# Row norms of a gated network's last layer split in two steps, and the first scores of an attention moved in front of other products

## The chip, the core and the metric

The kernel runs on one core of one Trainium2 chip. A core has five engines with a queue each: TensorE (PE, matrix products; its weight loads are listed apart as PEld), VectorE (DVE), ScalarE (ACT), GpSimd (POOL) and SyncE (SP, which here only issues DMAs). Each engine is given its instructions in an order that is fixed when the program is built; where one needs the result of another engine, it waits. The metric is the time on the device in microseconds (us) of one execution; the figure is the median of several runs.

## What is computed

The reference is a two-layer network on x of shape (8, 256, 512). Each layer adds a gated cross-attention on a context and then a gated feed-forward block, each behind a layer norm:

```python
x = x + tanh(g_xattn[0]) * _L0_xattn_ref(_layernorm(x), ctx, ctx)
x = x + tanh(g_ffn[0])   * _L0_ffn_ref(_layernorm(x), ...)
x = x + tanh(g_xattn[1]) * _L1_xattn_ref(_layernorm(x), ctx, ...)
x = x + tanh(g_ffn[1])   * _L1_ffn_ref(_layernorm(x), ...)
```

The change touches the second layer only. Its attention projects the queries (a linear with bias, then an RMS norm) and runs a softmax attention of 16 heads of 32 over 256 keys of each of the 8 batches. Its feed-forward block norms a row once more, rounds it to 8 bits with a scale from the row's largest magnitude, multiplies it with ternary weights, forms `value * silu(gate)`, rounds that in the same way and projects it back:

```python
h  = x * rsqrt(mean(x * x) + EPS) * w_norm
gv = _bitlinear(h, w_gv)            # scale from max(abs(h)) of each row
out = _bitlinear(value * silu(gate), w_out)
return x + out
```

## The kernel before

The 2048 rows of x are 16 tiles of 128 rows, two for each of the 8 batches (blocks b = 0 to 7). The program has three parts: the preparation of layer 0's weights with layer 1's keys and values, then layer 0's feed-forward, then layer 1's feed-forward. Each part interleaves the attention of later or earlier blocks with its own work. The last part, from about 750 us on, is the one that the change touches.

**How the order is set.** Every step (a Python function that issues some instructions) gets a place by hand: `at(b, (n, step))` puts it at block b plus n/16, and `timeline` (L617) issues all steps in the order of their places. One block of layer 1 is 16 places long, one for each `glu` step. On TensorE this written order is kept exactly: `pe.held` (L860) chains each matmul behind the one before. On the other engines a planner in the compiler reorders: it plays the program through in its own model of time and lets each engine take, of the instructions that it believes ready, the one written first. `behind(ins, last)` (L301) adds an order between two instructions of one engine, with no semaphore; the planner must then keep them in that order.

**What one block does** (places in sixteenths of a block, in the repeating middle):

- `Feed1.glu(k)` (L1252), places 0 to 15: eight steps for each of the two tiles. A step multiplies the tile's transposed 8-bit rows (zT) into a PSUM bank pair, which ACT copies to `gv` (L1269). Every second step ACT forms a tanh (L1273, tile `t`), and DVE does three instructions: L1274 and L1276 (the tile `u`) and L1277 (its largest magnitude).
- `Feed1.done` (L1309), from 8.6 for the first tile and 17.4 (so 1.4 of the next block) for the second: the scale (L1286 to L1289, small DVE instructions), two ACT instructions on `u` (L1315), two on POOL (L1316), DMA transposes (L1321), and 16 matmuls into a bank `py`. The first tile of a block uses the bank named "o" for it, the second the one named "py". `store` (L1302) adds the result to x (L1306 on DVE), which frees the bank, and sends the rows out. The first tile's second half of these matmuls stands at 18.2, so at 2.2 of the next block.
- `Feed1.ready` (L1211), norms of the next block's tiles, written as one step `norm` at 10.3 (first tile) and 13.0 (second) and a step `turn` 1.7 later. `norm` takes the moments on DVE, two reciprocal roots on POOL (through `rsqrt`, L269), y and z on POOL (L1220, L1226); then on DVE the row's largest magnitude (`amax`, L1228), the scale (L1229 to L1231) and the rounding (L1233, and L1234 to `zq`); then on POOL the residual (L1236, L1237) and three 128x1 products (`back`, L1242 to L1244). `turn` sends zq through a transposing DMA on SP into zT.
- `Attention1.ready` (L1050), three blocks ahead: a layer norm at 3.6, its transposes at 12.2, the queries' first linear (`normed.first(0)`) at 14.2, the second at 16.2 (0.2 of the next block; 15.6 for the first such attention), their scale at 0.5, the loads of keys and values at 1.0 and the transposes to `qT` at 2.9. Both linears write the one bank "py", one after the other: the second can't start before DVE has added the bias of the first (L756), and ACT squares the sum (L757) behind it. The transposes go to a PSUM pair `turned`, which ACT copies to qT (L348).
- `Attention.looks`, two blocks ahead: for each of four groups of heads, `scores(g)` runs the products of qT and kT (16 matmuls of 32 rows, into two PSUM pairs) and takes their negated maxima with two DVE reductions (L419, `nm`). The places are 4.4, 6.4, 7.4 and 9.3; `parts` and `shift` follow at 10.4 and 14.1.
- `Attention.weighs`, one block ahead: `exps(g)` (scores again, the other way round, with the maxima added, then ACT's exponentials at L485) at 15.2 of the block before, 1.2, 3.4 and 5.6, and `weigh(g)` (products with the values, into the bank "o") at 3.2, 4.2, 6.2 and 7.2.
- `Attention1.done`: 7.3 to 11.2, the division by the sums and the output projection.

The PSUM pairs with the tag "s" are two buffers in turn: `turned` takes one, and `scores` and `exps` take both. All matmuls have line L257 and all of these transposes L260, since `Tensor` issues them; they are told apart by their tiles. "s<-kT,qT" is `scores`, "s<-qT,kT" is `exps`.

The last three blocks differ: from block 5 on no new queries are begun, from block 6 on there are no more scores, and block 7's tiles are normed at 7.7 and 8.4 of block 6.

Of the kernel before, what the change touches and what calls it, by code (L numbers as in the profile page):

```python
# [45 lines left out]
ALU = mybir.AluOpType  # L46
AX = mybir.AxisListType
# [40 lines left out]
def flamingo_kernel(  # L88
# [24 lines left out]
    nc = tc.nc  # L113
# [32 lines left out]
    def want(i, n):  # L146
        assert stage.get(i, 0) == n, (i, n)
# [48 lines left out]
    for g in range(DC):  # L196
        for i in range(2):
            at = SR * g + SR // 2 * i
# [63 lines left out]
    pe = Tensor()  # L262

    exp = [None]


    block = {}
# [33 lines left out]
    def behind(ins, last):  # L301

        if last is not None:
            tc.add_manual_dep(
                ins.ins,
                last.ins.name,
                mybir.DependencyInfo(mybir.DependencyClass.NoSync, mybir.DependencyReason.DATA),
                reason="behind",
            )
        return ins  # L310
# [31 lines left out]
    def turned(srcs, dst):  # L342

        t = pair((P, 2, DC, P), name="turned")
        for i, src in enumerate(srcs):
            for c in range(DC):
                pe.transpose(t[:, i, c, :], src[:, c * P : (c + 1) * P], ident)
        nc.scalar.copy(dst.rearrange("p c (i t) -> p i c t", i=2), t)  # L348
# [13 lines left out]
    class Attention:  # L362
# [3 lines left out]
        n = 0  # L366
# [185 lines left out]
    class Attention0(Attention):  # L552
# [3 lines left out]
        def ready(self):  # L556
            def load():
                self.kT = self.new("kT", [DC, S])
                nc.sync.dma_start(out=self.kT, in_=cxT[self.b].rearrange("(c p) s -> p c s", p=P))
                self.v = self.new("v", [2, D])  # L560
                nc.sync.dma_start(out=self.v, in_=cx[self.b].rearrange("(k p) d -> p k d", p=P))

            def norm():

                rows = [xs[2 * self.b], xs[2 * self.b + 1]]
                self.y = layernorm(rows, att, "y", float(HD), block.get("V"))

            def turn():
                self.qT = self.new("qT", [DC, S])
                turned(self.y, self.qT)  # L570

            return self.counted(0, [load, norm, turn])
# [52 lines left out]
    def at(b, *steps):  # L625

        return [(b + n / 16, b + n / 16, [step]) for n, step in steps]
# [116 lines left out]
    def normed(src, w, bias, nw, dst, pool, tag, out2):  # L744

        st = {}

        def first(i):
            if i == 0:
                st["ss"] = small.tile([P, 2], F32, tag="ss", name="ss")  # L750
                st["t"] = []
                st["out"] = out2()
            t = pool.tile([P, D], F32, tag=tag, name="lin", bufs=YB)
            out = st["out"](i)
            linear(out, src(), i, w)
            nc.vector.tensor_tensor(t, out, bias(), ALU.add)  # L756
            nc.scalar.activation(junk, t, AF.Square, accum_out=st["ss"][:, i : i + 1])  # L757
            st["t"].append(t)

        def scale():  # L760
            r = rsqrt(st["ss"], 2, 1.0 / D, 1e-6)
            for i, t in enumerate(st["t"]):
                if nw is None:
                    nc.gpsimd.tensor_scalar(t, t, r[:, i : i + 1], 0.0, ALU.mult, ALU.add)
                else:
                    nc.vector.scalar_tensor_tensor(t, t, r[:, i : i + 1], nw(), ALU.mult, ALU.mult)

        def turn():
            turned(st["t"], dst())

        return [lambda: first(0), lambda: first(1), scale, turn]
# [48 lines left out]
    with ExitStack() as part:  # L820
# [16 lines left out]
        jobs = []  # L837
# [3 lines left out]
        for b in range(B):  # L841
            load, k0, k1, scale, turn, store, v0, v1 = kv[b]
# [280 lines left out]
    with ExitStack() as part:  # L1123
# [4 lines left out]
        def rows(b):  # L1128
# [3 lines left out]
        jobs = [  # L1132
            (0.5, 3.0, [lambda u=u: measure1(u) for u in range(n1)]),
            (3.05, 3.05, [scales1]),
            (3.1, 6.5, [lambda u=u: quantize1(u) for u in range(n1)]),
            (6.6, 6.6, [hold1]),
            (3.0, 3.0, [load_queries]),
        ]
# [66 lines left out]
    class Feed1:  # L1205
# [3 lines left out]
            self.i = i  # L1209

        def ready(self):  # L1211
            def norm():
                xt = xs[self.i]
                want(self.i, 3)
                mv = moments([xt])
                m, var = mv[:, 0, 0:1], mv[:, 0, 1:2]
                r = rsqrt(var, 1, 1.0, LN_EPS)[:, 0:1]
                nc.vector.tensor_scalar_mul(m, m, -1.0)
                y = work.tile([P, D], F32, tag="yr", name="yr", bufs=2)
                nc.gpsimd.tensor_scalar(y, xt, m, r, ALU.add, ALU.mult)  # L1220

                v2 = small.tile([P, 1], F32, tag="v2", name="v2")
                nc.vector.scalar_tensor_tensor(v2, r, r, var, ALU.mult, ALU.mult)
                r2 = rsqrt(v2, 1, 1.0, 1e-5)[:, 0:1]
                z = work.tile([P, D], F32, tag="z", name="z", bufs=2)
                nc.gpsimd.tensor_tensor(z, y, nw, ALU.mult)  # L1226
                amax = small.tile([P, 1], F32, tag="amax", name="amax")
                nc.vector.tensor_reduce(amax, z, AX.X, ALU.max, apply_absolute_value=True)  # L1228
                nc.vector.tensor_tensor(amax, amax, r2, ALU.mult)  # L1229
                sc, inv = scale8(amax)  # L1230
                nc.vector.tensor_tensor(sc, sc, r2, ALU.mult)  # L1231
                self.zq = work.tile([P, D], BF, tag="zq", name="zq", bufs=2)
                nc.vector.tensor_scalar(z, z, sc, MAGIC, ALU.mult, ALU.add)  # L1233
                nc.vector.tensor_scalar_add(self.zq, z, -MAGIC)  # L1234

                nc.gpsimd.tensor_scalar(y, y, tg[:, 3:4], 0.0, ALU.mult, ALU.add)  # L1236
                nc.gpsimd.tensor_tensor(xt, xt, y, ALU.add)  # L1237


                self.back = small.tile([P, 3], F32, tag="back", name="back")  # L1240
                back = self.back
                nc.gpsimd.tensor_tensor(back[:, 0:1], inv, winv[:, 0:1], ALU.mult)  # L1242
                nc.gpsimd.tensor_tensor(back[:, 1:2], inv, whalf, ALU.mult)
                nc.gpsimd.tensor_tensor(back[:, 2:3], back[:, 0:1], back[:, 1:2], ALU.mult)  # L1244

            def turn():
                self.zT = work.tile([P, DC, P], BF, tag="zT", name="zT", bufs=3)
                nc.sync.dma_start(out=self.zT, in_=self.zq, transpose=True)

            return [norm, turn]  # L1250

        def glu(self, k):  # L1252
            if k == 0:
# [30 lines left out]
        def scale(self):  # L1284
            amax = small.tile([P, 1], F32, tag="amax", name="amax")
            nc.vector.tensor_reduce(amax, self.amax, AX.X, ALU.max)  # L1286
            nc.vector.tensor_tensor(amax, amax, self.back[:, 2:3], ALU.mult)
            sc, self.inv = scale8(amax)
            nc.vector.tensor_tensor(sc, sc, self.back[:, 2:3], ALU.mult)  # L1289
            self.uq = work.tile([P, HID], BF, tag="uq", name="uq", bufs=1)  # L1290
            return sc
# [69 lines left out]
    jobs = []  # L1361
    for b in range(B):
        first, second, a = feed1[2 * b], feed1[2 * b + 1], att1[b]
        end = b == B - 1
        jobs += at(b, *((k, step) for k, step in enumerate(first.glus() + second.glus())))

        far = {B - 1: (15.95, 15.95), B - 2: (15.95, 15.95), B - 3: (13.2, 17.3)}.get(b, (13.2, 18.2))
        steps = {B - 1: (7.05, 7.1, 7.15), B - 2: (7.4, 9.6, 9.8)}.get(b, (8.6, 9.6, 9.8))
        jobs += at(b, *zip((*steps, *far), first.done()))
        if end:  # L1370
            jobs += at(b, (16.0, second.last))
        else:
            far = {B - 2: (31.9, 31.9), B - 3: (21.2, 22.2)}.get(b, (21.2, 24.2))
            jobs += at(b, *zip((17.4, 18.4, 18.6, *far), second.done()))
        if b >= 2:

            late = 15.6 if b == 2 else 16.2
            jobs += at(b - 3, *zip((3.6, 12.2, 14.2, late, 16.5, 17.0, 18.9), a.ready()))
            jobs += at(b - 2, *zip((4.4, 6.4, 7.4, 9.3, 10.4, 14.1), a.looks()))
        if b >= 1:  # L1380
            steps = (-0.8, 0.6, 2.3, 2.5, 3.2, 3.4, 4.2, 5.0) if end else (-0.8, 1.2, 3.2, 3.4, 4.2, 5.6, 6.2, 7.2)
            jobs += at(b - 1, *zip(steps, a.weighs()))
        steps = (5.1, 6.9, 7.6, 8.2) if end else (7.3, 9.2, 10.2, 11.2)
        jobs += at(b - 1, *zip(steps, a.done()))
        for n, f in zip((7.7, 8.4) if end else (10.3, 13.0), (first, second)):
            norm, turn = f.ready()
            jobs += at(b - 1, (n, norm), (n + 1.7, turn))
    timeline(*jobs)


# [50 lines left out]
```

## Time and profile before

| | |
|---|---|
| median of 3 runs | 1191.43 us (1191.4 to 1193.26) |
| the profiled execution's own time | 1192.33 us |
| its span, first to last instruction | 1190.6 us |
| mean granted TensorE clock | 0.987 |
| PE busy in the span | 1092.7 us, 92% |
| DVE, ACT, POOL busy | 791.4, 598.0 and 495.1 us |
| one block of layer 1 in the middle (872.3 to 932.0) | 59.7 us, PE busy 57.0, DVE 46.4, ACT 31.5, POOL 26.7 |

The profile is of one execution. In a row of its timeline stand the start and the length in us, the engine, the line, the operation, the tiles (written <- read), the shape and the count; in brackets the idle time of the engine ahead of it, and the instruction that ended this. In the view of waits a row names who waited for whom, with the total in us, the number of times and the longest. The end of a matmul is modelled, so a neighbour can start a tenth of a microsecond before it. Times below are counted from the start of the span.

### The profile page before, as it was taken

To read this page: it belongs to the slowest core of one execution; us is meant where nothing else is said; L and a number is where in the kernel's file an instruction comes from. 1 tells how busy PE (TensorE), PEld (TensorE's weight loads), DVE (VectorE), ACT (ScalarE), POOL (GpSimd) and SP (SyncE) were. 2 spreads that over 40 slices of the span, in tenths; PEclk is the share of its full clock that TensorE was granted. 3 is DMA by queue.
4 is the path that set the end of the run, shared out by engine and by line. 5 is a ranking of instruction groups with operands and counts; after the bars stand their busy time and mean duration, and the time that the engine had idled before them with its cause. 6 is when DMAs were issued, how large, how long until landed. Compare 5 with 4: busy or idle time off the path is not lost.

```text
span 1190.6 us, 31314 instructions
## 1 busy us (share of the span) xinstructions
PE 1092.7 (92%) x13290; PEld 738.2 (62%) x13389; DVE 791.4 (66%) x1612; ACT 598.0 (50%) x1060; POOL 495.1 (42%) x792
## 2 busy tenths in 40 slices
PE   5899998999999989988999998998999999999987
PEld 1445446777777767776667775565656565656654
DVE  5686986745647375655656445687878787868585
ACT  3466554466665434344443542536363646464654
POOL 3112112543435475565645226544444444424250
PEclk9999999999999999999999999999999999999999
DMA  8444435523433233242311114011122122211212
GB/s 300 142 161 160 146 138 182 156 90 109 107 109 99 65 93 99 82 101 90 83 50 42 20 37 159 25 44 49 50 49 51 45 55 45 55 32 31 44 41 57
DMA packets 99469, 104.08 MB, mean 87 GB/s; under 512 B 60992, under 2 KB 72320, under 8 KB 99328
## 3 DMA queue, kind: packets, MB, share of 16 engines
q1 hardware_dynamic: 95728, 96.03, 27.8%
q10 hardware_dynamic: 3600, 6.03, 1.6%
q8 instruction: 105, 1.72, 0.6%
q14 instruction: 36, 0.29, 0.1%
HBM read 72.09 MB, written 15.73 MB: 74 GB/s over the span
## 4 chain that ended last, share of the span: by engine, by line
PE 34%; DVE 26%; POOL 17%; ACT 11%; issue 9%; DMA 3%; DVEq 0%; POOLq 0%; SPq 0%; ACTq 0%
PE gu L257 9%; PE o L257 6%; PE lin L257 6%; PE s L257 5%; DVE nm L419 4%; PE y L257 3%; ACT h L919 2%; POOL rs_r L274 2%; DVE h L912 2%; DMA xT<-yp 2%; DVE h L911 2%; PE py L257 2%; POOL hs L299 2%; POOL acc L921 2%; ACT hs L916 2%
## 5 line engine op out<-in xcount | busy, mean ns | idle before, releaser
L257 PE MATMUL gu<-xT,gu 128*128 128x128 f16 x4096 | 256.4, 222 | 10.5 <-DMA xT<-yp 6.8
L257 PEld LDWEIGHTS <-gu 128*128 128x128 bf16 x4096 | 238.9, 99 | 40.8 <-issue 18.0
L274 POOL TENSOR_TENSOR rs_r<-rs_t,mhalf 128x1 f32<-128x1 f32 (+1 forms) x88 | 61.9, 705 | 212.7 <-DVE rs_t L272 200.9
L257 PE MATMUL gu<-gv,zT 128*128 128x256 fp8e4 x1024 | 131.7, 275 | 6.0 <-ACT gv L1269 4.6
L921 POOL TENSOR_TENSOR acc<-acc,h 128x256 f32<-128x256 f32 x112 | 82.7, 739 | 114.9 <-ACT h L919 113.0
L257 PEld LDWEIGHTS <-zT 128*128 128x128 bf16 x1024 | 96.4, 98 | 51.8 <-issue 36.5
L1269 ACT COPY gv<-gu 128x512 f32<-128x512 f32 x128 | 74.0, 584 | 95.6 <-PE gu L257 75.3
L916 ACT CAST hs<-h 128x256 f16<-128x256 f32 x128 | 51.7, 404 | 138.7 <-DVE h L912 137.9
L257 PE MATMUL y<-pr,hs 128*128 128x512 bf16 x413 | 113.0, 381 | 6.2 <-DVE x L963 0.6
L485 ACT ACTIVATE p<-s 128x768 f32<-128x768 f32 (+1 forms) x128 | 109.5, 906 | 16.0 <-PE s L257 15.5
L911 DVE SCALAR_TENSOR_TENSOR h<-h,gu 128x256 f32<-128x256 f32 x128 | 53.2, 416 | 95.4 <-ACT h L910 95.2
L919 ACT ACTIVATE h<-h,hid 128x256 f32<-128x256 f32 x112 | 56.7, 508 | 67.4 <-POOL hs L299 41.3
L419 DVE TENSOR_REDUCE nm<-s 128x4 f32<-128x1024 f32 x64 | 75.7, 1219 | 21.8 <-PE s L257 21.8
L299 POOL TENSOR_TENSOR hs<-h,hs 128x256 f16<-128x256 f32 x64 | 43.7, 683 | 100.2 <-ACT hs L916 100.2
L1274 DVE SCALAR_TENSOR_TENSOR t<-t,gv 128x512 f32<-128x512 f32 x64 | 48.3, 754 | 45.9 <-ACT t L1273 45.9
L257 PE MATMUL s<-qT,kT 32*128 32x256 f32 (+1 forms) x1024 | 74.9, 372 | 2.6 <-DVE rs_t L272 1.6
L910 ACT ACTIVATE h<-gu 128x256 f32<-128x256 f32 x128 | 48.4, 378 | 50.4 <-PE gu L257 49.9
L257 PE MATMUL s<-kT,qT 32*128 32x256 f32 (+1 forms) x1024 | 68.9, 374 | 2.3 <-ACT p L485 1.9
L257 PE MATMUL lin<-wk,cT 128*128 128x512 f32 x128 | 61.0, 621 | 9.8 <-DMA wk<-in_k_wT_dram 9.8
L411 DVE TENSOR_REDUCE nm<-s 128x2 f32<-128x256 f32 (+1 forms) x128 | 62.8, 552 | 8.9 <-PE s L257 8.9
L257 PE MATMUL o<-p,v 128*32 128x256 f32 (+1 forms) x1024 | 61.7, 358 | 6.9 <-DVE x L1306 4.9
L522 POOL TENSOR_TENSOR oT<-oT 128x128 f32<-128x128 f32 x48 | 26.6, 555 | 98.4 <-ACT oT L519 98.4
(180 smaller groups left out, 2070.5 us busy)
## 6 DMA issues: line engine op xcount, KB each, us to landing
w<-in_gvT_dram SPq DMA_DIRECT2D x32, 512.0 KB
w<-in_guT_dram SPq DMA_DIRECT2D x16, 512.0 KB
w<-in_outT_dram SPq DMA_DIRECT2D x16, 512.0 KB
cT<-in_cxT_dram SPq DMA_DIRECT2D x8, 512.0 KB
x<-in_x_dram SPq DMA_DIRECT2D x16, 256.0 KB
kT<-in_cxT_dram SPq DMA_DIRECT2D x8, 512.0 KB
v<-in_cx_dram SPq DMA_DIRECT2D x8, 512.0 KB
kd<-k SPq DMA_DIRECT2D x8, 512.0 KB
```

The source lines that it names most:

```text
L257: return self.kept(nc.tensor.matmul(*args, **kwargs))
L274: nc.gpsimd.tensor_tensor(r[:, :n], t[:, :n], mhalf[:, :n], ALU.pow)
L299: (nc.vector if engine == "V" else nc.gpsimd).tensor_tensor(dst, a, b, op)
L411: nc.vector.tensor_reduce(nm[:, :, qb], s[j][:, :, at[qb] : at[qb] + to[qb]], AX.X, ALU.max, negate=True,)
L419: nc.vector.tensor_reduce(nm, s[j].rearrange("p r (q k) -> p r q k", q=2), AX.X, ALU.max, negate=True)
L485: exp[0] = nc.scalar.activation(self.p[j], s[j][:, :, 0:n], AF.Exp)
L910: block["A"] = nc.scalar.activation(h, gu[:, 0], AF.Tanh, scale=0.5 / UP0)
L911: nc.vector.scalar_tensor_tensor(h, h, 1.0, gu[:, 0], ALU.add, ALU.mult)
L916: nc.scalar.copy(hs[:, 0], h)
L919: nc.scalar.activation(sq, h, AF.Square, scale=hid[:, 1:2])
L921: block["P"] = nc.gpsimd.tensor_tensor(self.acc[i], self.acc[i], sq, ALU.add)
L1269: nc.scalar.copy(self.gv[:, :, k % 2, :], gu)
```

## The change

`norm` of `Feed1.ready` is cut in two at the `amax` reduction: `norm` keeps what stands before it, and a new step `scale` holds the rest, down to the three `back` products. It is placed 0.05 behind `norm`, but 1.35 behind it for the second tile of a block (14.35, after the queries' first linear at 14.2); for the last block's two tiles it stays at 0.05. The `amax` reduction is ordered behind the bias addition L756 that was written last when the step is issued (`biased[0]`). For a second tile that is the first linear of the same block's queries, where the block has any; for the other tiles it is one issued long before. The first scores of an attention move from 4.4 to 3.1, which puts them behind the transposes to qT (2.9) and `glu(3)` and in front of `weigh(0)` (3.2), `exps(2)` (3.4), `glu(4)` and `weigh(1)` (4.2). No instruction is added or removed.

```diff
+    biased = [None]
...
-            nc.vector.tensor_tensor(t, out, bias(), ALU.add)
+            biased[0] = nc.vector.tensor_tensor(t, out, bias(), ALU.add)
...
         def ready(self):
+            st = {}
+
             def norm():
...
                 nc.gpsimd.tensor_tensor(z, y, nw, ALU.mult)
+                st.update(xt=xt, y=y, z=z, r2=r2)
+
+            def scale():
+                xt, y, z, r2 = (st[k] for k in ("xt", "y", "z", "r2"))
                 amax = small.tile([P, 1], F32, tag="amax", name="amax")
-                nc.vector.tensor_reduce(amax, z, AX.X, ALU.max, apply_absolute_value=True)
+                behind(
+                    nc.vector.tensor_reduce(amax, z, AX.X, ALU.max, apply_absolute_value=True),
+                    biased[0],
+                )
...
-            return [norm, turn]
+            return [norm, scale, turn]
...
-            jobs += at(b - 2, *zip((4.4, 6.4, 7.4, 9.3, 10.4, 14.1), a.looks()))
+            jobs += at(b - 2, *zip((3.1, 6.4, 7.4, 9.3, 10.4, 14.1), a.looks()))
...
-            norm, turn = f.ready()
-            jobs += at(b - 1, (n, norm), (n + 1.7, turn))
+
+            late = 1.35 if f is second and not end else 0.05
+            jobs += at(b - 1, *zip((n, n + late, n + 1.7), f.ready()))
```

## The prediction

> **What bounds the kernel now.** I read the page first, then the waits of TensorE (PE) from 805 to 1062 us, where the touched steps repeat, then the timeline there.
>
> ```profile
> PE 1092.7 (92%) x13290; PEld 738.2 (62%) x13389; DVE 791.4 (66%) x1612; ACT 598.0 (50%) x1060; POOL 495.1 (42%) x792
> ```
>
> PE is the bound, so only its idle time can be won. In the repeating stretch that is three waits (total, times, longest), and no others:
>
> ```profile
> PE lin L257 <- DVE lin L756: 6.8, 5, 2.6
> PE o L257 <- DVE x L1306: 4.9, 5, 1.0
> PE inv L257 <- DVE x L1306: 2.2, 4, 0.6
> ```
>
> The stretch repeats every 59.7 us (the same matmul at 867.82, 927.50 and 987.20). One repetition around the first wait, out of the timeline:
>
> ```profile
> 866.74 0.43 DVE L1234 TENSOR_SCALAR zq<-z 128x512 bf16<-128x512 f32 x1
> 867.08 0.68 DVE L756 TENSOR_TENSOR lin<-lin,rqb 128x512 f32<-128x512 f32 x1
> 867.80 0.63 ACT L757 ACTIVATE junk<-lin 128x512 bf16<-128x512 f32 x1 [7.14 <-DVE lin L756]
> 867.82 3.70 PE L257 MATMUL lin<-wq,xT 128*128 128x512 f32 x8 [1.03 <-DVE lin L756]
> ```
>
> The first linear ended at 863.63, but its bias (L756) stood on VectorE (DVE) behind the second tile's scale chain (L1228 to L1234, 863.64 to 867.17). ScalarE (ACT) lost 7.14 us there, PE 1.03. The second wait, and all that the second edit touches:
>
> ```profile
> 876.54 1.09 PE L260 MATMUL turned<-ident,lin 128*128 128x128 f32 x8
> 877.29 2.36 ACT L1315 ACTIVATE u<-u,magic,s 128x1024 f32<-128x1024 f32 x2
> 877.47 1.04 PE L257 MATMUL gu<-gv,zT 128*128 128x256 fp8e4 x8
> 879.48 1.07 PE L257 MATMUL o<-p,v 128*32 128x256 f32 x16 [0.98 <-DVE x L1306]
> 879.55 0.58 ACT L1269 COPY gv<-gu 128x512 f32<-128x512 f32 x1
> 880.01 1.03 ACT L348 COPY qT<-turned 128x1024 f32<-128x1024 f32 x1
> 882.31 0.69 DVE L1274 SCALAR_TENSOR_TENSOR t<-t,gv 128x512 f32<-128x512 f32 x1 [2.88 <-ACT t L1273]
> 885.51 1.15 PE L257 MATMUL s<-kT,qT 32*128 32x256 f32 x16
> 886.69 2.36 DVE L419 TENSOR_REDUCE nm<-s 128x4 f32<-128x1024 f32 x2 [0.56 <-PE s L257]
> ```
>
> See that the scores (885.51) run long after their qT (ready 881.04), and that qT stands on ACT behind L1315 and a gv copy, though its transposes ended at 877.63. ACT follows the written order here (positions 1.2, 1.4, 2.0, 2.9, 3.0).
>
> **Part one, the tie.** Nothing is added but the order. L756 now runs at 863.7 to 864.4, PE is free for the second linear at 866.79 (865.74 + 1.05), so its wait goes: 1.03 in each of four blocks and 2.63 at 808.12, the 6.8 of the view. Behind L756 come the chain's seven instructions (3.53), so zq comes at 867.9 instead of 867.17. The transposing DMA on SP goes out 0.7 late; SP's next issue is at 879.90 and its reader is half a block away. POOL's three 128x1 products for "back" (0.19, 0.19, 0.25) wait as long, and POOL is then idle (7.82 before 874.57). Cost nothing, unless 10 us of cover go. In block -1 the amax (751.57) stood behind L756 (748.90) already, and for the last four tiles the tied instruction is long past: nothing there.
>
> What is late next is ACT. On DVE the second L756 follows the chain, L1274/1276/1277 (0.69 each) and five small ones (871.95 to 872.93, 0.98): 864.4 + 3.53 + 2.07 + 0.98 = 871.0, or 870.6 if the planner puts it ahead of the small ones (its linear ends at 866.79 + 3.70). Before it was 872.85. The square on ACT starts 0.71 later (873.56), the exponentials 1.92 after that (875.48; now not before 872.66, when their scores end), and qT ends 5.56 after those (881.04). So **qT is ready at 878.8 to 879.2; I take 879.0**, 2.0 earlier than before, while PE comes 1.17 earlier (1.03, and the 0.14 that the transposes waited for ACT at 876.54).
>
> [...] The 128x1 product L1231 took 0.93 here (865.22), 0.15 at 1106.10. [...]
>
> **Part two, the scores in front.** PE follows the written order, so it is now: transposes, glu 3, first scores, first products, second exponentials' scores, glu 4. Glu 3 ends at 877.3 (878.51 - 1.17). The scores wait for qT at 879.0: **1.7 us of wait take the place of the 0.98** at 879.48 (L1306, then done long before). The scores' own 1.08 and the products' 1.88 (879.48 to 881.36) only change places. No DMA or POOL work moves; SP and POOL are not passed. The reduces' readers (parts, 10.4) are far off.
>
> Next, exps(2) needs both PSUM pairs, which the scores now hold until both reduces (L419, 1.22 each) are done. With Tq for qT's end, PE gets to exps(2) at Tq + 3.0 (0.05 + 1.08 + 1.88). The reduces could start at Tq + 1.25, but glu 3's L1274 is ready at Tq + 1.3 (881.04 to 882.31), L1276 and L1277 behind it. The order was set by the planner; the trace of before does not show it, so I bound it. The second reduce ends at
> - d, both reduces first: Tq + 3.6 (1.25 + 2.36)
> - a, one reduce, L1274, one reduce: Tq + 4.3
> - b, L1274, reduce, L1276, reduce: Tq + 5.1
> - c, all of L1274, L1276 and L1277 ahead of the second reduce: Tq + 5.8
>
> After it exps(2) takes 1.34 (770.34 to 771.68, where the same wait shows). Against glu 4 at 882.66 before, and less the scores' 1.08 that no longer follow: d +0.2, a +0.9, b +1.7, c +2.4 us per block, the gains of both edits included. I take b, by this view of DVE:
>
> ```profile
> 899.89 0.10 DVE L1286 TENSOR_REDUCE amax<-umax 128x1 f32<-128x4 f32 x1
> 900.03 0.16 DVE L1287 TENSOR_TENSOR amax<-amax,back 128x1 f32<-128x1 f32 x1
> 900.11 1.22 DVE L419 TENSOR_REDUCE nm<-s 128x4 f32<-128x1024 f32 x1
> 901.25 0.14 DVE L1200 TENSOR_SCALAR s8i<-amax 128x1 f32<-128x1 f32 x1
> 901.31 1.22 DVE L419 TENSOR_REDUCE nm<-s 128x4 f32<-128x1024 f32 x1
> ```
>
> Those scores had ended at 898.52 (897.37 + 1.15), and L1286 is written after them (8.6 against 7.4): the planner believed them over 1 us later than they are, and wove the two reduces between dependent instructions.
>
> **Sum.** Blocks 2 to 5: 4 x 1.7 = 6.8. Block 1, which loses 2.63 instead of 1.04 of wait: 1.7 - 1.6 = +0.1. Block 0, where part one wins nothing: qT ends at 761.13, glu 4 was at 763.95, so 761.13 + 5.1 + 1.34 - 763.95 - 1.08 = +2.5, less the waits of 0.34 and 0.43 at 769.26 and 770.39 for these same reduces: +1.8. Together **+8.7 us**. The profiled execution took 1192.33 (span 1190.6); the median of the runs is 1191.43, 0.9 less. Against the median: 1200.1.
>
> **Rivals.**
> - d: reduces first. 4 x 0.2 - 1.4 + 0.3 = -0.3, 1191.1: no change. For it: scores end before t by the durations here. Against: the planner's late scores. Chance 0.13.
> - a: 4 x 0.9 - 0.7 + 1.0 = +3.9, 1195.3. Chance 0.22.
> - c: 4 x 2.4 + 0.8 + 2.5 = +12.9, 1204.3. For it the same late scores. (The next norm's two L281 ahead as well, 1.28 a block more, is left out of the range.) Chance 0.18.
> - Faster: qT's copy goes ahead of the two L1315. Transposes end at 875.4 + 1.09, qT at 877.5, the scores wait 0.2; gv and t then come after L1315, so the reduces are first: 877.5 + 3.6 + 1.34 - 882.66 - 1.08 = -1.3 per block, 4 x -1.3 - 2.9 + 0.3 = -7.8, 1183.6; with L1274 between, -4.3, 1187. It decides if L1315's factor (L1289, 872.78) comes later than the exponentials, 4 us of slack away in the trace. Chance 0.17. That the tie does nothing would only take 6.8 from the gains, and the idle 7.14 on ACT speaks against it.
>
> **Numbers.** b has 0.30, so 1200.1. The range takes in a, b, c and d, c with qT 0.4 later (5 x 0.4): 1206.3, and the near end of the faster case: 1187 to 1207. Under 0.2% (2.4 us, about what a measurement tells from no change) lies d: faster 0.17, same 0.13, slower 0.70.
>
> **What would show it.** Right: PE waits lin <- L756 and o <- L1306 gone from 805 to 1062; ACT's 7.14 down to about 3.8; a new wait of s for L348 (qT) of 1.5 to 1.9, or 0.3 in block 0; one of s for L419 of 0.6 to 2.8; blocks of 60 to 62 us. The inv wait stays. Wrong: qT's copy ahead of L1315, or both L419 directly behind the scores with no L1274 between; then the block is shorter than 60 us.

## The result, and the profile after

The changed kernel takes 1217.68 us (median of four, 1217.31 to 1218.62) beside 1191.51 for the kernel before on the same chip: a ratio of 1.0224, 95% interval 1.0208 to 1.024. It is **26 us slower**. 1200.1 was predicted, in a range that ended at 1207: the sign was right, the size three times too small.

The profiled execution took 1217.31 us, with a span of 1215.6 (before: 1192.33 and 1190.6) and a mean granted clock of 0.979 (0.987). The new lines shift the numbers: L756 is now L758, L1269 L1280, L1274 to L1277 are L1285 to L1288, L1306 is L1317, L1315 L1326, L281 L283, L348 L350, L419 L421. The page's first part:

```profile
PE 1107.7 (91%) x13389; PEld 741.5 (61%) x13389; DVE 786.8 (65%) x1612; ACT 598.3 (49%) x1060; POOL 491.0 (40%) x792
```

Not one instruction was added. That the row of before has 99 matmuls fewer (13290) is a gap in its profile, all of them `y<-pr,hs` in the parts ahead of the one that the change touches, so the 15.0 us by which the two rows differ are not all of this change. From the same matmul on (`lin<-wq,xT`, 744.62 before and 742.50 after) both profiles hold 4116 matmuls: this stretch grew from 445.98 to 473.10 us, by 27.1, and PE is busy for 413.31 of it before and for 425.37 after. So some 12 us are matmuls that took longer, and 15 are idle time. Next the waits of PE from 805 to 1062 us (total, times, longest):

```profile
PE s L257 <- DVE nm L421: 12.6, 8, 2.1
PE s L257 <- ACT qT L350: 6.7, 4, 1.7
PE inv L257 <- DVE x L1317: 3.7, 4, 0.9
```

Two of the three old waits are gone (lin, 6.8, and o, 4.9). Two of s, 19.3 us together, stand in their place, and that of inv went from 2.2 to 3.7. ACT in the repeating block, out of its timeline:

```profile
871.92 0.63 ACT L759 ACTIVATE junk<-lin 128x512 bf16<-128x512 f32 x1 [3.74 <-DVE lin L758]
...
882.23 2.37 ACT L1326 ACTIVATE u<-u,magic,s 128x1024 f32<-128x1024 f32 x2
...
884.96 1.03 ACT L350 COPY qT<-turned 128x1024 f32<-128x1024 f32 x1
```

The first linear's square waits 3.74 instead of 7.14, and qT still stands behind L1326 and a gv copy. It ends at 885.99. PE and then DVE, directly behind it:

```profile
886.04 1.15 PE L257 MATMUL s<-kT,qT 32*128 32x256 f32 x16 [1.67 <-ACT qT L350]
...
891.18 0.70 PE L257 MATMUL s<-qT,kT 32*128 32x256 f32 x4 [2.12 <-DVE nm L421]
892.90 0.48 PE L257 MATMUL s<-qT,kT 32*128 32x256 f32 x2 [1.02 <-DVE nm L421]
...
894.43 1.89 PE L257 MATMUL gu<-gv,zT 128*128 128x256 fp8e4 x8
```

```profile
887.26 0.69 DVE L1285 SCALAR_TENSOR_TENSOR t<-t,gv 128x512 f32<-128x512 f32 x1 [2.89 <-ACT t L1284]
887.99 0.69 DVE L1287 TENSOR_TENSOR u<-t,gv 128x512 f32<-128x512 f32 x1
888.71 0.69 DVE L1288 TENSOR_REDUCE umax<-u 128x1 f32<-128x512 f32 x1
889.32 0.68 DVE L283 BATCH_NORM_STATS2 ln_st<-x 128x6 f32<-128x512 f32 x1
889.91 1.21 DVE L421 TENSOR_REDUCE nm<-s 128x4 f32<-128x1024 f32 x1
891.04 0.68 DVE L283 BATCH_NORM_STATS2 ln_st<-x 128x6 f32<-128x512 f32 x1
891.64 1.21 DVE L421 TENSOR_REDUCE nm<-s 128x4 f32<-128x1024 f32 x1
```

The scores end at 887.19, but their first reduction starts at 889.91: four instructions stand ahead of it on DVE, glu 3's three and one statistic of the next layer norm (L283), and the other statistic stands between the two reductions. DVE worked through all of this without idling; only its order holds PE up. The second exponentials' scores (s<-qT,kT) can go on only behind each of these reductions, so PE waits 2.12 and then 1.02.

The last row of PE is a second finding. glu 4's eight matmuls took 1.05 before, and take 1.89 here, though nothing kept them waiting. The row of before:

```profile
882.66 1.05 PE L257 MATMUL gu<-gv,zT 128*128 128x256 fp8e4 x8
```

Stretches of the timeline after (stretch, length, then busy time of PE, PEld, DVE, ACT and POOL, the granted clock, DMA):

```profile
882.45:947.01 64.56, 58.83 (x579) 37.07 (x578) 45.59 (x90) 31.63 (x47) 25.40 (x41) 0.97 0.19 46
893.80:897.40 3.60, 3.60 (x26) 1.70 (x26) 0.00 (x0) 2.52 (x3) 3.49 (x5) 0.53 0.00 0
897.40:900.00 2.60, 2.60 (x51) 1.96 (x44) 0.00 (x0) 0.78 (x2) 1.23 (x2) 1.00 0.02 6
```

**The clock fell to a half for 3.4 us (893.88 to 897.3) behind these waits, and then came back.** The block is 64.56 us long; it was 59.70, at a clock of 1.00.

### The profile page after: what moved, and what is told of

It is laid out like the page before. It is cut to its first block, busy times and chain, and to the rows that moved or that the text cites. A ratio compares the mean times of both kernels' runs of the same rounds, so it can differ in the third digit from the quotient of the medians.

```text
span 1215.6 us, 31399 instructions
## 1 busy us (share of the span) xinstructions
PE 1107.7 (91%) x13389; PEld 741.5 (61%) x13389; DVE 786.8 (65%) x1612; ACT 598.3 (49%) x1060; POOL 491.0 (40%) x792
## 4 chain that ended last, share of the span: by engine, by line
PE 47%; DVE 22%; POOL 12%; ACT 12%; issue 4%; DMA 2%; DVEq 0%; SPq 0%; POOLq 0%; ACTq 0%
PE gu L257 14%; PE lin L257 9%; PE s L257 6%; PE o L257 5%; DVE nm L421 4%; PE y L257 3%; PE proj L257 3%; PE py L257 3%; POOL acc L923 2%; ACT h L921 2%; ACT p L487 2%; DVE h L914 2%; POOL w L1030 2%; POOL hs L301 2%; DVE h L913 2%
## 5 line engine op out<-in xcount | busy, mean ns | idle before, releaser
L257 PE MATMUL gu<-gv,zT 128*128 128x256 fp8e4 x1024 | 136.9, 282 | 6.2 <-ACT gv L1280 4.8
L257 PE MATMUL y<-pr,hs 128*128 128x512 bf16 x512 | 131.6, 380 | 0.6 <-DVE x L965 0.6
L1280 ACT COPY gv<-gu 128x512 f32<-128x512 f32 x128 | 73.3, 584 | 94.1 <-PE gu L257 89.2
L1285 DVE SCALAR_TENSOR_TENSOR t<-t,gv 128x512 f32<-128x512 f32 x64 | 47.2, 737 | 79.6 <-ACT t L1284 79.4
L257 PE MATMUL s<-qT,kT 32*128 32x256 f32 (+1 forms) x1024 | 80.4, 379 | 18.6 <-DVE nm L421 17.2
L421 DVE TENSOR_REDUCE nm<-s 128x4 f32<-128x1024 f32 x64 | 75.3, 1211 | 20.9 <-PE s L257 20.9
L257 PEld LDWEIGHTS s<-qT,kT 32*128 32x128 f32 x1024 | 43.1, 188 | 38.1 <-DVE nm L421 21.5
```

Of the source, the lines that this page charges most:

```text
L257: return self.kept(nc.tensor.matmul(*args, **kwargs))
L421: nc.vector.tensor_reduce(nm, s[j].rearrange("p r (q k) -> p r q k", q=2), AX.X, ALU.max, negate=True)
L1280: nc.scalar.copy(self.gv[:, :, k % 2, :], gu)
```

## The experiments

My theory after reading this: part one wins what it was costed at, and part two loses it three times over, through the place of qT on ACT, the place of the reductions on DVE, and the clock. The rival: the tie itself moves DVE's planned order, and the reductions come late for that. Against both stands a third, that the clock alone makes the difference between 8.7 and 26.

**Each part alone.** First the tie without the scores' move; then the move without the tie, on the kernel before.

```diff
-            jobs += at(b - 2, *zip((3.1, 6.4, 7.4, 9.3, 10.4, 14.1), a.looks()))
+            jobs += at(b - 2, *zip((4.4, 6.4, 7.4, 9.3, 10.4, 14.1), a.looks()))
```

> The tie and the split norm alone; the first scores stay at place 4.4. Theory (the whole loss sits in the moved scores, the tie is a gain): the waits of TensorE for L756's bias (6.8 us in all) and nearly all of its waits for the store ahead of the first products (4.9) go, 59.7 us a block become 57.5 to 58.6, and the time 1180 to 1186 us. Rival (the later scale chain on VectorE is part of the loss): slower than before, 1194 to 1205 us, with new waits on VectorE in each block.

Measured: 1178.71 us, ratio 0.9892 (0.9877 to 0.9907). All waits of PE from 805 to 1062:

```profile
PE o L257 <- DVE x L1317: 2.2, 5, 1.0
PE inv L257 <- DVE x L1317: 2.2, 4, 0.6
```

The lin wait is gone, the store's wait (o) is down from 4.9 to 2.2, and a block is 57.36 long. The tie alone wins 13 us, so with the scores at their old place the tie does not make the reductions late; whether it does with the move is for the next run.

The move alone, in the kernel before:

```diff
-            jobs += at(b - 2, *zip((4.4, 6.4, 7.4, 9.3, 10.4, 14.1), a.looks()))
+            jobs += at(b - 2, *zip((3.1, 6.4, 7.4, 9.3, 10.4, 14.1), a.looks()))
```

> The moved first scores alone, in the kernel before. Theory: in each block the scores wait 2.5 us for qT (881.0 against 878.5 before), the second exponentials' scores about 3.1 us for the two reductions, the granted clock falls to a half for some 3.4 us behind that, and the store's wait of 0.98 goes: 6 to 7 us a block, 1220 to 1228 us. Rival (the tie makes the loss, by putting the row norm's statistics between the reductions): 1186 to 1195 us.

Measured: 1233.26 us, ratio 1.0346 (1.0328 to 1.0363); blocks of 68.0. Its waits over the same stretch:

```profile
PE s L257 <- DVE nm L419: 12.1, 8, 2.1
PE s L257 <- ACT qT L348: 10.4, 4, 2.6
PE inv L257 <- DVE x L1306: 3.7, 4, 0.9
PE lin L257 <- DVE lin L756: 3.0, 4, 0.8
```

The waits for the reductions are those of the changed kernel (12.1 beside 12.6), so they come with the move, whatever the tie does. With this the rival falls. The move costs 41.6 us alone and 39.0 behind the tie; the two parts nearly add (-12.9 and +41.6 give +28.7, beside the +26.2 of both). It cost more than I had expected because the clock was halved for 6.83 us in every block here, not for 3.41.

**Is it the tie or only the place of the scale?** The first kernel again, the scale still a step of its own at the later place, but not ordered behind anything:

```diff
-                behind(
-                    nc.vector.tensor_reduce(amax, z, AX.X, ALU.max, apply_absolute_value=True),
-                    biased[0],
-                )
+                nc.vector.tensor_reduce(amax, z, AX.X, ALU.max, apply_absolute_value=True)
```

> The split norm with the second tile's scale at 14.35, without the order behind L756; the first scores at 4.4. Theory (what helps is the order on VectorE, and the planner, which believes the scale's inputs ready before the linear, keeps it ahead of L756 wherever it is written): as before, 1189 to 1194 us, with the second linear's waits of 1.03 and 2.63. Rival (the later place is enough): 1176 to 1182 us.

Measured: 1190.55 us beside 1191.33, ratio 0.9997 (0.9987 to 1.0007), with the waits of the kernel before (lin 6.8, o 4.9, inv 2.2). The later place alone does nothing; the 13 us come only with the order.

**qT earlier.** Three steps of the second tile's `done` (its quantizing and its two transposing DMAs) are placed later, and its two ACT instructions, which are ordered behind `exp[0]`, come behind the qT copy:

```diff
-        nc.scalar.copy(dst.rearrange("p c (i t) -> p i c t", i=2), t)
+        exp[0] = nc.scalar.copy(dst.rearrange("p c (i t) -> p i c t", i=2), t)
...
-            jobs += at(b, *zip((17.4, 18.4, 18.6, *far), second.done()))
+            steps = (18.95, 19.5, 19.7) if b < 5 else (17.4, 18.4, 18.6)
+            jobs += at(b, *zip((*steps, *far), second.done()))
```

> The changed kernel with the second tile's quantizing step at 18.95 instead of 17.4 in blocks 0 to 4 and its ScalarE instructions (L1315 before) ordered behind the copy to qT. Theory (the late copy begins the loss): the scores' wait for qT falls from 1.67 to about 0.3; the planner now puts one reduction ahead of glu 3's instruction on t, which itself comes late, so exps(2) still waits about 2.3; no half clock; about 4.8 us a block less, 1190 to 1200 us. Rival (the copy's place is unimportant, only the reductions' place behind glu 3 and the norm counts): the wait moves from the copy to the reductions in full, 1212 to 1218 us.

Measured: 1204.43 us, ratio 1.011 (1.0095 to 1.0125); blocks of 61.6. The wait for qT is down to 0.23, and one wait of 1.71 for the reductions is left. That was half of the matter: the time lies between the theory's range and the rival's, since the clock was still halved for 3.41 us in every block, behind one wait of 1.71.

**The reductions first.** glu 3's three DVE instructions are ordered behind the first scores' reductions:

```diff
+                if k == self.later:
+                    self.rest = rest
+                else:
+                    rest()
...
+            f = feed1[2 * (b - 2)]
+            f.later = 3
+            jobs += at(b - 2, (3.15, lambda f=f: f.rest(maxed[0])))
```

> The changed kernel with glu 3's three VectorE instructions (on t, u and umax) ordered behind the first scores' two reductions. Theory (the loss is qT's wait, plus reductions that stand behind those three and one of the norm's statistics, plus the half clock that the long wait brings): the reductions' wait falls from 2.12 and 1.02 to about 0.6 in all, the clock stays at 1.00, qT's wait of 1.67 stays, and the block is 59.5 to 60.5 us, 1190 to 1197 us. Rival (the half clock comes from the first wait or from the order of the products): 1200 to 1205 us, with the half clock in each block.

Measured: 1191.79 us, ratio 1.0001 (0.9991 to 1.001). No wait for nm is left; those for qT are (2.59, 1.67, 1.67, 1.90, 1.90). Blocks are 61.64, 59.71, 59.34 and 60.57 long. All waits of PE from 805 to 1062:

```profile
PE s L257 <- ACT qT L352: 9.7, 5, 2.6
PE inv L257 <- DVE x L1328: 2.9, 4, 0.9
```

The order on DVE is thus shown to be what makes the 12.6 us of nm waits. The clock, which the theory had at 1.00, fell behind the waits of 2.59 and 1.90, and not behind those of 1.67. PE is busy 58.1 us in the blocks where it fell and 57.1 in the others.

**Both edits together.**

> Both: the copy to qT ahead of the second tile's quantizing on ScalarE, and the two reductions ahead of glu 3's instructions on VectorE. Theory (with both conditions met the scores in front cost next to nothing, but win nothing over the tie alone, since TensorE had no idle time to fill there beyond 0.31): the waits are 0.2 and 0.6 to 0.7, no half clock, 58 to 59 us a block, 1180 to 1187 us. Rival (the scores in front are worth something once their inputs are there): below the tie alone, under 1177 us. Other rival (the half clock stays): 1190 us or more.

Measured: 1181.59 us, ratio 0.9915 (0.99 to 0.993), blocks of 57.9 to 58.4. The waits are 0.23 to 0.34 for qT and 0.55 to 0.92 for inv, with no stretch at half clock in blocks 0 to 5. With both queues put right the move costs no more than 2.9 us over the tie alone; it still wins nothing. What it stays behind by is inv and some 0.6 of PE time a block.

**The norm's share.** Only the next layer norm is ordered behind the reductions, so that L283 can't go ahead of them:

```diff
-                self.y = layernorm(rows, att, "y", last=block.get("V"))
+                self.y = layernorm(rows, att, "y", last=maxed[0] if "py" in part_ps else block.get("V"))
```

> The changed kernel with the statistics of the next layer norm (written at 3.6) ordered behind the first scores' reductions; glu 3's three instructions stay ahead. Theory: the second reduction ends 1.3 us earlier, so the waits fall from 2.12 and 1.02 to about 1.8 in all; whether the half clock goes with it decides between 1208 to 1211 us (it stays) and 1200 to 1204 us (it goes). Rival (the statistics were not in the way): 1216 to 1219 us.

Measured: 1204.19 us, ratio 1.0108 (1.0093 to 1.0123). The waits for the reductions fall from 2.12 + 1.02 to 1.52 + 0.43. That is 1.19 a block for the two L283. Of blocks 1 to 4 only 1 and 3 show the half clock here, which is why the time lies between the two cases that were expected, and which prices it. Blocks 1 to 4, columns as in the stretches above:

```profile
818.29:881.05 62.76, 58.86 (x578) 37.49 (x579) 46.74 (x92) 32.47 (x48) 25.28 (x41) 0.97 0.19 47
881.05:942.86 61.81, 57.26 (x580) 36.57 (x579) 45.83 (x90) 31.52 (x47) 25.28 (x41) 1.00 0.20 48
942.86:1005.91 63.05, 58.86 (x579) 37.14 (x578) 44.28 (x89) 31.41 (x46) 25.82 (x41) 0.97 0.19 47
1005.91:1067.57 61.66, 57.25 (x579) 36.57 (x578) 44.65 (x90) 31.61 (x48) 25.81 (x41) 1.00 0.24 48
```

Compare the blocks at 0.97 with their neighbours at 1.00: the same work, and PE busy 1.6 us longer. The blocks are longer by less, 62.76 - 61.81 = 0.95 to 63.05 - 61.66 = 1.39 us, because those at 0.97 have less idle time (3.90 and 4.19 beside 4.55 and 4.41). So the half clock costs 1.6 us a block here.

**Filling the wait.** To tell the clock from the waits, PE is given useless work in the gap: glu 4's eight matmuls are issued once more into their own bank, ahead of the second exponentials' scores. The second kernel issues them twice more.

```diff
+            jobs += at(b - 2, (3.3, lambda f=feed1[2 * (b - 2)]: f.twice(4)))
```

> The changed kernel, with the eight matmuls of glu(4) issued twice in blocks 0 to 5: once more between the first products and the second exponentials' scores, into the same bank, so that TensorE is idle there for 1.1 us less. The result is the same. Theory (the granted clock falls because TensorE idles too much within one stretch): the clock stays at 1.00 in blocks 1 to 4, glu(4) takes 1.05 again instead of 1.89, and the time is 1208 to 1212 us although 6 x 1.04 us of matmuls are added. Rival (the clock falls for another reason, or the loss is not in it): the added matmuls lie in the wait and change nothing, 1216 to 1219 us, with the half clock in the same place.

Measured: 1214.13 us, ratio 1.0184 (1.0168 to 1.0201). This lies between the two ranges. The nm waits are 1.14 + 1.02 (0.61 in block 1), so the extra set ran inside the wait. Blocks: 63.84 (clock 0.97), 65.82 (0.95, half clock for 6.83 us), 63.23 (1.00), 64.19 (0.97). The clock came back in one block of four.

> The changed kernel with the matmuls of glu(4) issued three times in blocks 0 to 5, the two added ones in the wait ahead of the second exponentials' scores; the result is the same. Theory (TensorE's idle time brings the half clock): of the first wait some 0.1 us is left, none of blocks 1 to 5 shows a half clock, 62.9 us a block, 1207 to 1211 us although 12 x 1.04 us of matmuls are added. Rival (the half clock hangs on something else): as with one added set, 1213 to 1216 us.

Measured: 1208.87 us, ratio 1.0145 (1.0126 to 1.0164), with waits of 0.26 + 1.02 (none in block 1); blocks 63.96 (0.97), 62.74 (1.00), 64.28 (0.97), 62.84 (1.00). The time came out as expected, but the reason did not wholly: two of the four blocks still show the half clock. PE is busy 1.3 to 1.6 us longer in these, which agrees with the 1.6 above. That eight and sixteen matmuls too many in a block make this kernel faster than the changed one shows that the listed waits are not all of its loss. The third theory, that the clock is the whole difference, falls: blocks at full clock are still 61.7 to 61.8 long with the norm behind (and 62.7 to 63.2 with the added matmuls), beside 59.70 before.

## Why the prediction was wrong, point by point

- **Part one.** Right in its mechanism. 1.03 and 0.14 a block were costed; the tie alone shortens the block by 59.70 - 57.36 = 2.34, of which 0.67 is the store's wait (0.98 to 0.31), which the prediction took off with the second edit. ACT's wait is 3.74 (about 3.8 predicted). The 128x1 product that had taken 0.93 took 0.19 (873.21). Before, POOL's addition (864.87 to 866.13) ran beside it; here that addition, 871.50 to 872.77, was over before it started. That the one made the other longer is not shown by this.
- **"1.7 us of wait take the place of the 0.98."** Right: 1.67, and 0.34 in block 0.
- **"b, L1274, reduce, L1276, reduce: Tq + 5.1."** This is the step that failed: the order on DVE, and so the wait of the second exponentials' scores. The second reduction ended 6.86 behind qT (885.99 to 892.85), later even than c (5.8). The order was L1285, L1287, L1288, L283, reduction, L283, reduction: more than c, and with it the case that was named (both L281 ahead as well) and then "left out of the range" without a reason. The view it rested on had shown the planner taking the scores for over 1 us later than they are; the right reading was that everything that is ready and written nearby goes ahead of them, not one instruction at a time between. Waits of 3.14 instead of about 2.1 for b followed. The later end, 6.86 instead of 5.1, is 1.8 of the 3.2 us a block by which the sum was short (4.9 instead of 1.7).
- **A term was missing: the clock.** The kernel before ran this stretch at 1.00, even behind its wait of 2.63 at 805.49, so the sum took all matmuls at their durations of before. In the changed kernel every block from 0 to 4 holds a stretch at half clock, which costs about 1.6 us by the table below, as in the blocks with the norm behind.
- **"The inv wait stays."** Wrong: 0.56 became 0.92. The trace shows where: on DVE the same thirteen instructions, from the t of glu 7 to the store's addition to x for which inv waits, take 6.88 us (909.00 to 915.88) instead of 6.51 (896.98 to 903.49). The small ones of the scale now stand in a row, and no longer between the two reductions.
- **Rivals.** "Faster: qT's copy goes ahead of the two L1315" did not happen; made by hand, it gave 1204.43 and not 1183.6, since the reductions did not come first by themselves. The prediction was right that DVE decides; it had taken for granted that a late gv would free DVE for them. With both made by hand (1181.59) the 1183.6 is nearly met.

From glu 3 to glu 3, a block accounts for itself so, in us:

| step | before to after |
|---|---|
| the second linear starts earlier; the transposes no longer wait for ACT | -1.2, -0.3 |
| the store's wait gone | -0.98 |
| the wait for qT | +1.67 |
| the wait ahead of the second exponentials' scores | +2.19 |
| these scores, in two pieces (1.02 of it a listed wait, some 0.3 the half clock from 893.88 on) | +1.95 |
| glu 4 and weigh 1 at half clock | +0.85, +0.48 |
| inv | +0.36 |
| sum (measured: 64.56 - 59.70 = 4.86) | +5.0 |

Blocks 1 to 4 were predicted at +0.1, +1.7, +1.7, +1.7, and block 0 at +1.8. They came out at +3.3 for block 1, +4.9 for the next three, and about +6.4 for block 0, which has waits of 2.12 and 0.51 and the clock at a half for twice as long, 6.83 us. Block 5 had 1.9 (predicted 1.7): its planned order has no L283 between, its waits are 1.53 and 0.43, and its clock stayed at 1.00 behind them. So where the order came close to the one that was costed, the price did too. These sum to 26.3, and the rest of the 27.1 comes behind block 5. The span grew by 2.1 less, since the profiled run reached this part of the program that much earlier than before, ahead of anything the change touches; in the eleven traces that matmul lies between 741.9 and 746.3, and the runs don't explain why.

**What stays open.** Why the clock falls behind some half-busy stretches of PE and not behind others; why block 1 waits 2.59 for qT in four of the kernels (the one ordered reductions first, the one with the norm behind them, and both with filled waits); and by what the planner chose its orders on DVE.

## What to carry to other kernels

When a step is moved forward, follow the whole way to the next user of its buffers: here not the scores were dear (their matmuls only changed places) but the two reductions that free their PSUM pair, and what a planner with its own idea of time puts ahead of these. An order between two instructions changes that (13 us won by one tie, 12.6 us of waits removed by another), while a later place in the written order changed nothing. And count a new TensorE wait as its length plus something for the clock, when it falls: here it fell behind some waits of 1.61 to 2.59 us and not behind others, and that made the matmuls of a block 1.0 (the reductions first) to 1.6 us (the norm behind) longer.

## What the runs showed of the hardware

The granted clock was halved for stretches of 3.41 us, or twice that, behind short waits: of 1.61 us (the tie alone, 1086.77 to 1088.38, half clock from 1090.01), of 1.71 in every block (qT earlier), of 1.90 and 2.59 (reductions first). It was not halved behind 1.67 in two blocks of that last kernel, nor behind 2.63 in the kernel before (805.49 to 808.12, 1.00 in the stretch after). The length of the wait alone does not decide, then.

The half stretches keep a grid of their own. In the changed kernel those of blocks 1 to 4 start at 829.03, 893.88, 958.74 and 1023.59, so 64.85 apart, which is 19 times the 3.413 that each of them is long in the trace, while the blocks are 64.56 to 64.60 long. Of the 15 half stretches of this trace (23.48 to 1214.73) and the 10 of the kernel before (32.33 to 1189.45), every one starts a whole number of such lengths behind the one before it. So PE's busy time can be counted in windows of this grid, and a wait can fall into one or be shared by two; that the clock is decided window by window was the author's assumption, and the runs show only how the two went together:

| kernel | window | PE busy, of 3.41 us | wait in it | clock behind it |
|---|---|---|---|---|
| before | 803.74 to 807.15 | 1.75 | 1.66 of the 2.63 | 1.00 |
| before | 807.15 to 810.57 | 2.45 | the other 0.97 | 1.00 |
| changed | 883.64 to 887.06 | 1.75 | 1.67 | 1.00 |
| changed | 890.47 to 893.88 | 1.68 | 0.71 of the 2.12, and 1.02 | half |
| changed | 1020.18 to 1023.59 | 2.25 | 0.13 of the 2.12, and 1.02 | half |
| reductions first | 813.11 to 816.52 | 1.25 | 2.16 of the 2.59 | half |
| tie alone | 1086.59 to 1090.01 | 1.81 | 1.61 | half |

The 2.63 of the kernel before is cut in two by the grid. From 750 us to the last matmul the eleven traces have 1383 such windows at full clock. All 25 in which PE was busy for less than 1.4 us were followed by half clock, and none of the 1250 in which it was busy for 2.3 or more; of the 108 between, 25 were. (The traces of before and changed alone have 251: 6 of 6, none of 224, and 4 of 21.) Where in between it falls is not settled by the busy time: 1.75 kept the clock, 1.81 and 2.25 lost it.

In the changed kernel three waits come within 8.5 us (884.37 to 892.90: 1.67, 2.12 and 1.02). But with qT earlier, a wait of 1.71 was followed by half clock in a block whose other wait ahead of it was 0.23, so these runs do not show that several waits are needed.
